# Layer 0 of a four-layer graph network: keys projected directly in turned form, their lengths moved into the exponentials, queries normed one block ahead

## The chip, the cores and the metric

The kernel runs on one core of a Trainium2 chip. The metric is the device time of one execution in microseconds (us). The kernel before takes 2383.84 us, the median of three runs from 2383.57 to 2384.07.

The engines are named as in the profile: PE does matmuls (PEld is its weight load), DVE is the vector engine, ACT the scalar engine, POOL is GpSimd, and SP issues nearly all transfers (DMA).

## The reference

Four layers are applied to 3327 nodes with 256 features each, under one 0/1 adjacency matrix. Each layer ends in a residual sum and a layer norm. All is fp32.

```python
# layer 0                                   x = layernorm(x + layer0(x, adj, Wq, Wk))
Qn = cos_normalize(x @ Wq.T)                # 3327 x 128, each row divided by max(its length, 1e-4)
Kn = cos_normalize(x @ Wk.T)
att = softmax(where(adj > 0, Kn @ Qn.T, -9e15), axis=1)
prop = att @ x                              # rows without a neighbour keep x
out = 0.5 * prop + 0.5 * x
# layer 1: graph attention, exp of leaky_relu(src_i + dst_j), times h = x @ W, then elu
# layer 2: scaled dot-product attention under the mask, q, k, v with biases, then elu
# layer 3: h = x @ W0, then three graph attention layers like layer 1
```

What matters here is layer 0. The row index i of the attention belongs to Kn and the summed index j to Qn. The kernel's code calls the i side queries and the j side keys, so its keys come from Wq and its queries from Wk. Each score is k_i . q_j / (|k_i| |q_j|).

## The kernel before

**Tiles and blocks.** The nodes are padded to 3328: 26 tiles of 128 (`NT`). A block (`b`) is four tiles, 512 rows of the attention; there are seven, the last with 256 rows. A group of tiles is the same four tiles seen as keys. Each of the six attention layers (`layers`: "0", "1", "2", "3a", "3b", "3c") is a loop over blocks, and in each block over the 26 key tiles `j`: one step of the flat list `steps`.

**One step of layer 0** (`weights0`, L438). PE multiplies the stationary `FT[j // 4][:, 0, ...]` (keys, turned: 128 features x 128 nodes) with the moving `FT[b][:, 1]` (queries, turned: 128 features x 512 nodes) into a PSUM bank `ps` (L444). ACT takes the exponential (`ex`, L453). DVE multiplies with the mask (`e`, L433). PE multiplies pieces of `e` with the features `V[0][j]` into four accumulators `po`. `make_to` makes steps ahead: while PE does the products of step `j`, the scores of step `j + 2` are made (`LA = 2`). For every second `j`, a 512 KB piece of the adjacency (`stage`, three buffers) has been loaded; DVE or ACT turn it into the byte mask, and DVE adds it up into `acc` (L405) to find rows without neighbours.

**Two forms of products.** Block 0 and the last block multiply plainly (L1253: four products of 257 columns a step). Blocks 1 to 5, and all of layer 2, use Strassen's scheme on pairs of tiles: `sums` makes four sums of `e` pieces on DVE (L656 to L659), `products` does 14 products of 128 or 129 columns a pair (L708). The sums of feature tiles that this needs (`tsum`) are made once per pair by `combine` (L629) on DVE, stored to memory (`t_d`, L640) and fetched again for each block (`fetch_tsum`, `tsums`, three buffers). In layer 0 `combine` runs at steps 9 to 21 of block 0; in layer 2 the sums of the last pair are made when the last block of layer 1 is finished, during block 0 of layer 2.

**Preparing layer 0** (`prep0(g)`, L286), a generator that is advanced a part at a time between the steps of block 0, for all seven groups. For each tile, two matmuls with `xT` stationary and 256 columns of weights moving give keys and queries side by side (`pqk`, L311); a copy brings them to SBUF (`qk`); ACT or DVE sum the squares (L302, L306); DVE takes the roots of eight columns at once (`rsqrt`, three Newton steps, eleven instructions, behind a maximum); DVE scales the queries (L346) and ACT the keys (L344); PE turns both (`pqkT`, L352) and ACT copies them to `FT` (L356). So every `ps` of a group stands behind its copy, squares, root, scaling and turn.

**Order.** Up to step 3 the order on PE, ACT, DVE and POOL is that of the program (`manual_schedule`). After that, and for SP throughout, Tile's scheduler orders each engine's instructions: by their place in the program, but by the times it expects for each, so an instruction it holds ready can be put ahead of one that it expects to wait. [...]The trace shows the effect on SP, where loads that the program issues in later blocks (`w_l_wq`, `a_3a`) stand at 33 to 40 us.

**Shared buffers.** The tag `x4k` has two buffers of 4 KB a partition. In block 0 of layer 0 it carries `xT` (the features turned, 512 KB a group) and the 13 `tsum` tiles; in later blocks of the layer it carries `y4`, the result that `finish` works on. The PSUM pool `ps_b` has three banks for everything except the accumulators.

Of the kernel before, what the change touches and what calls it, by code (L numbers as in the profile page):

```python
# [19 lines left out]
P = 128  # L20
D = 256
H = 128
# [11 lines left out]
def gnn_stack(ctx: ExitStack, tc: tile.TileContext, a: dict, N: int, out: bass.AP):  # L34
# [15 lines left out]
    def bw(b):  # L50
        return min(CH, NP - b * CH)

    def tiles_of(b):
        return range(4 * b, min(4 * b + 4, NT))
# [11 lines left out]
    def bank(name):  # L66
        return ps_b.tile([P, CH], F32, tag="pb", name=name)
# [61 lines left out]

    w = {}  # L130

    def rsqrt(dst, v, n):

        g = cols.tile([P, n], I32, tag="rs_g", name="rs_g")
        nc.vector.tensor_scalar(g, v.bitcast(I32), -0.5, MAGIC, ALU.mult, ALU.add)
        y = g.bitcast(F32)
        vh = cols.tile([P, n], F32, tag="rs_v", name="rs_v")
        nc.vector.tensor_scalar(vh, v, -0.5, None, ALU.mult)
        for k in range(3):
            q = cols.tile([P, n], F32, tag="rs_q", name="rs_q")  # L140
            nc.vector.tensor_tensor(q, y, y, ALU.mult)
            nc.vector.tensor_tensor(q, q, vh, ALU.mult)
            z = dst if k == 2 else cols.tile([P, n], F32, tag="rs_y", name="rs_y")
            nc.vector.scalar_tensor_tensor(z, q, 1.5, y, ALU.add, ALU.mult)
            y = z


# [123 lines left out]
    def load_xT(g):  # L271
        wd = bw(g)
        xT = work.tile([P, 2, CH], F32, tag="x4k", name="xT", bufs=2)
        src = a["xT"].rearrange("(h p) n -> p h n", p=P)
        if g == 0:
            for q, c in ((nc.scalar, 0), (nc.sync, D)):
                q.dma_start(xT[:, :, c : c + D], src[:, :, c : c + D])
        else:
            nc.sync.dma_start(xT[:, :, :wd], src[:, :, g * CH : g * CH + wd])
        xTs[g] = xT  # L280

    def load_x(g):
        for t in tiles_of(g):
            nc.sync.dma_start(V[0][t][:, :D], a["x"][t * P : (t + 1) * P, :])

    def prep0(g):  # L286

        wd = bw(g)
        xT = xTs[g]
        ts_ = tiles_of(g)  # L290
        ss = cols.tile([P, 2, 4], F32, tag="ss", name="ss")
        if len(ts_) < 4:
            nc.vector.memset(ss, 1.0)
        qks = []

        def squares(k):
            for i in range(2):
                s = qks[k][:, i * H : (i + 1) * H]
                c = ss[:, i, k : k + 1]
                jk = work.tile([P, H], F32, tag=f"sq{i}", name=f"sq{i}", bufs=1)  # L300
                if g < 2 and i == 1:
                    nc.vector.tensor_tensor_reduce(  # L302
                        jk, s, s, 1.0, 0.0, ALU.mult, ALU.add, c
                    )
                else:
                    nc.scalar.activation(jk, s, AF.Square, accum_out=c)  # L306

        for k, t in enumerate(ts_):
            pm = bank("pqk")
            for h in range(2):  # L310
                nc.tensor.matmul(  # L311
                    pm[:, : 2 * H],
                    xT[:, h, k * P : (k + 1) * P],
                    w["qk"][:, h, :],
                    start=(h == 0),
                    stop=(h == 1),
                )
            tag, bufs = ("y", 6) if g % 2 else ("qk", 4)
            qk = work.tile([P, 2 * H], F32, tag=tag, name="qk", bufs=bufs)
            if g in (1, 2):  # L320
                nc.scalar.copy(qk, pm[:, : 2 * H])
            else:
                nc.vector.tensor_copy(qk, pm[:, : 2 * H])
            qks.append(qk)
            if g == 0:
                squares(k)
        yield
        if g > 0:
            for k in range(len(ts_)):
                squares(k)  # L330
            yield

        sf = ss.rearrange("p i k -> p (i k)")
        nc.vector.tensor_scalar(sf, sf, COS_EPS * COS_EPS, None, ALU.max)
        rn = cols.tile([P, 8], F32, tag="rn", name="rn")
        rsqrt(rn, sf, 8)
        if g == 1:
            yield
        for k in range(len(ts_)):
            for i in (1, 0):  # L340
                s = qks[k][:, i * H : (i + 1) * H]
                c = rn[:, 4 * i + k : 4 * i + k + 1]
                if i == 0:
                    nc.scalar.mul(s, s, c)  # L344
                else:
                    nc.vector.tensor_scalar(s, s, c, None, ALU.mult)  # L346
        yield
        for i in (1, 0):
            pt = bank("pqkT")
            for k, t in enumerate(ts_):  # L350
                s = qks[k][:, i * H : (i + 1) * H]
                nc.tensor.transpose(pt[:, k * P : (k + 1) * P], s, ident)  # L352
            if i == 1 and g == 0:
                nc.vector.tensor_copy(FT[g][:, i, :wd], pt[:, :wd])
            else:
                nc.scalar.copy(FT[g][:, i, :wd], pt[:, :wd])  # L356


    masks = {}
# [78 lines left out]
    def weights0(b, j):  # L438
        wd = bw(b)
        if j % 2 == 0:  # L440
            take_adj(b, j)
            load_adj()
        ps = bank("ps")
        nc.tensor.matmul(  # L444
            ps[:, :wd],
            FT[j // 4][:, 0, (j % 4) * P : (j % 4 + 1) * P],
            FT[b][:, 1, :wd],
            start=True,
            stop=True,
        )  # L450
        t_ = work.tile([P, CH], F32, tag="a", name="ex", bufs=3)

        nc.scalar.activation(t_[:, :wd], ps[:, :wd], AF.Exp)  # L453
        return masked(b, j, t_)

    gq = {}
# [169 lines left out]
    def strassen(L, b):  # L626
        return L.key == "2" or (L.key == "0" and 0 < b < NB - 1)

    def combine(key, p, v):  # L629

        b1, b2 = v[2 * p], v[2 * p + 1]
        b11, b12, b21, b22 = b1[:, H:D], b1[:, :H], b2[:, H:D], b2[:, :H]
        t = work.tile([P, 4 * H + 1], F32, tag="x4k", name="tsum", bufs=2)
        t1, t2, t3, t4 = (t[:, c : c + H] for c in (0, H + 1, 2 * H + 1, 3 * H + 1))
        nc.gpsimd.memset(t[:, H : H + 1], 1.0)
        nc.vector.tensor_tensor(t1, b12, b11, ALU.subtract)
        nc.vector.tensor_tensor(t2, b22, t1, ALU.subtract)
        nc.vector.tensor_tensor(t3, b22, b12, ALU.subtract)
        nc.vector.tensor_tensor(t4, t2, b21, ALU.subtract)
        nc.sync.dma_start(t_d[key][p], t)  # L640

    tsums = {}

    def fetch_tsum(key, b, p):
        t = work.tile([P, 4 * H + 1], F32, tag="tsum", name="tsums", bufs=3)
# [499 lines left out]
    def make(s):  # L1145
        if s >= len(steps):
            return
        L, b, j = steps[s]
        if strassen(L, b) and j % 2 == 0:
            fetch_tsum(L.key, b, j // 2)  # L1150
        if L.is_gat:
            made.append(L.gat.weights(b, j))
        else:
            made.append((weights0 if L.key == "0" else weights2)(b, j))
            if strassen(L, b) and j % 2:
                e2, e1 = made.pop(), made.pop()
                made.append(None)
                made.append(sums(b, e1, e2))
# [10 lines left out]
    load_x(0)  # L1169
    load_adj()  # L1170
    masks[0] = new_mask(0)
    prep = [prep0(0), prep0(1)]
    next(prep[0])
    next(prep[1])
    next(prep[0])
    next(prep[0], None)
    for s in range(LA):
        make(s)
    prep.pop(0)
    setup = setups()  # L1180
    pre = iter(())

# [4 lines left out]
    def make_to(n):  # L1187
        nonlocal upto
        while upto < n:
            make(upto)  # L1190
            upto += 1

    for s, (L, b, j) in enumerate(steps):
# [8 lines left out]
            pos = [ps_o.tile([P, wo], F32, tag="po", name="po") for _ in range(no)]  # L1202
        if first:

            g, part = (j + 4) // 4, j % 4
            if part == 2 and g + 1 < NB:
                load_x(g + 1)
                if g + 2 < NB:
                    load_xT(g + 2)
                prep.append(prep0(g + 1))  # L1210
                next(prep[-1])
                if g > 1:
                    next(prep[-1])
                else:
                    next(prep[0])
                    next(prep.pop(0), None)
            if j == 3:
                next(prep[0])
            if g < NB and g > 1 and part < 2:
                next(prep[0], None)  # L1220
                if part == 1:
                    prep.pop(0)
        if j == 0 and first:
            load_x(1)
            load_xT(2)
            make_to(s + LA + 1)
            next(prep[0])
        elif j == 1 and first:
            make_to(s + LA + 1)
            next(prep[0])  # L1230
        else:
            make_to(s + LA + 1 + extra)
        es = None if end else made.popleft()
        if end:

# [139 lines left out]
```

## Time and profile before

| | |
|---|---|
| runs | 2383.57 to 2384.07 us, median 2383.84 |
| profiled execution | 2386.34 us |
| its span (first to last instruction) | 2384.6 us |
| PE busy | 2349.7 us, 99% |
| DVE, ACT, POOL busy | 1618.4, 1212.8, 13.5 us |
| layer 0: first `ps`, first `po`, end of block 0 | 16.2, 18.9, 121.1 us |
| blocks 2, 3, 4 of layer 0 | 63.0 us each |
| moved by DMA | 212.83 MB, 89 GB/s on average |

A busy PE in this profile is not PE at its peak: matmul lengths overlap, and their ends are modelled. The pace of a run of matmuls is read from the starts of successive runs. A line of the order of time gives start, length, engine, source line, operation, output and inputs with their shapes, the count, and in brackets the idle time before it with what ended it. An fp32 matmul of the program appears as two matmul instructions, a transpose as one.

### The profile page before, as it was taken

What the parts mean: (1) busy time and instruction counts of PE and PEld (TensorE: products, weight loads), DVE (VectorE), ACT (ScalarE), POOL (GpSimd) and SP (SyncE); (2) the same over time, 40 slices, a digit from 0 to 9 for tenths busy, and PEclk for the clock granted to TensorE, in tenths of its full rate; (3) what the DMA queues carried; (4) which work ended last, traced back from release to release, by engine and by line L of the source; (5) the groups of instructions that cost most, each with busy time, mean ns of one, the idle gap of its engine ahead of it and who ended that gap; (6) DMA issues with size and microseconds to landing.
All of it is one profiled execution on the core that took longest, in us unless ns stands there. A gap on an engine that the chain in (4) does not pass through costs nothing.

```text
span 2384.6 us, 33057 instructions
## 1 busy us (share of the span) xinstructions
PE 2349.7 (99%) x11911; PEld 1916.7 (80%) x11911; DVE 1618.4 (68%) x4353; ACT 1212.8 (51%) x1984; POOL 13.5 (1%) x91
## 2 busy tenths in 40 slices
PE   9999999999999999999999999999999999999997
PEld 6687777888888776677667798888888888888886
DVE  6789999966666657567467585556656555655665
ACT  5666666665555422222222255565655555655554
POOL 0000000000000000000000000000000000000000
PEclk9999999999999999999999999999999999999999
DMA  7556555523223322222212231111221111132120
GB/s 228 165 167 191 183 186 181 175 82 94 73 69 70 100 56 87 67 69 84 64 62 72 76 93 47 55 65 34 61 62 43 43 52 51 47 100 69 60 66 23
DMA packets 146232, 212.83 MB, mean 89 GB/s; under 512 B 76061, under 2 KB 100884, under 8 KB 141460
## 3 DMA queue, kind: packets, MB, share of 16 engines
q1 hardware_dynamic: 145796, 210.45, 29.3%
q8 instruction: 94, 1.54, 0.3%
q14 instruction: 70, 0.57, 0.1%
q10 hardware_dynamic: 272, 0.26, 0.0%
HBM read 165.70 MB, written 28.19 MB: 81 GB/s over the span
## 4 chain that ended last, share of the span: by engine, by line
PE 64%; DVE 2%; ACT 1%; DMA 1%; issue 0%; POOL 0%; POOLq 0%; DVEq 0%; ACTq 0%
PE po L1253 36%; PE ps L506 12%; PE po L708 11%; PE pproj L917 3%; DMA turned<-planes 1%; PE pgq L465 1%; PE po L1238 1%; ACT re L600 1%; DVE e L611 0%; PE pv L1002 0%; DVE v L611 0%; ACT planes L763 0%; DVE ejunk L534 0%; DVE pT L773 0%; DMA u<-s_d 0%
## 5 line engine op out<-in xcount | busy, mean ns | idle before, releaser
L1253 PE MATMUL po<-v,e 128*128 128x257 f32 x5616 | 1251.7, 381 | 2.5 <-ACT p L886 1.7
L1253 PEld LDWEIGHTS po<-v,e 128*128 128x128 f32 x5616 | 1063.2, 190 | 174.9 <-issue 15.2
L600 ACT ACTIVATE re<-u,nrh,th 128x512 f32<-128x512 f32 (+1 forms) x728 | 555.9, 780 | 478.4 <-DVE e L611 474.9
L611 DVE SCALAR_TENSOR_TENSOR e<-re,rh,mask 128x512 f32<-128x512 f32 (+1 forms) x702 | 502.4, 719 | 380.1 <-PE po L1253 360.5
L433 DVE SCALAR_TENSOR_TENSOR e<-ex,mask 128x512 f32<-128x512 f32 (+1 forms) x364 | 234.8, 649 | 183.7 <-ACT ex L514 157.0
L506 PE MATMUL ps<-gT,ft 128*128 128x512 f32 (+1 forms) x728 | 307.7, 563 | 0.0
L514 ACT ACTIVATE ex<-ps,off 128x512 f32<-128x512 f32 (+1 forms) x182 | 119.2, 655 | 360.3 <-PE ps L506 331.5
L708 PE MATMUL po<-tsums,ssum 128*128 128x128 f32 (+1 forms) x1794 | 250.1, 275 | 2.6 <-DVE ssum L658 1.3
L708 PEld LDWEIGHTS po<-tsums,ssum 128*128 128x128 f32 x1794 | 224.3, 192 | 5.1 <-DVE ssum L658 2.3
L708 PEld LDWEIGHTS po<-v,e 128*128 128x128 f32 x1196 | 169.7, 191 | 71.3 <-issue 53.6
L506 PEld LDWEIGHTS ps<-gT,ft 128*128 128x128 f32 x728 | 131.9, 190 | 113.6 <-issue 110.7
L708 PE MATMUL po<-v,e 128*128 128x129 f32 x1196 | 183.2, 275 | 0.0
L453 ACT ACTIVATE ex<-ps 128x512 f32<-128x512 f32 (+1 forms) x182 | 102.7, 564 | 119.8 <-PE ps L444 106.3
L444 PE MATMUL ps<-ft,ft 128*128 128x512 f32 (+1 forms) x312 | 143.6, 568 | 0.8 <-ACT ft L356 0.7
L405 DVE CUSTOM_DVE_ANT_0 acc<-acc,stage 128x1024 uint16<-128x1024 uint16 (+1 forms) x168 | 109.0, 649 | 13.8 <-DMA stage<-in_adj_a 9.8
L708 PE MATMUL po<-v,ssum 128*128 128x128 f32 x598 | 92.3, 275 | 0.0
L708 PE MATMUL po<-tsums,e 128*128 128x128 f32 x598 | 92.1, 275 | 0.0
L397 ACT ACTIVATE mask<-pos 128x1024 uint8<-128x1024 bf16 (+1 forms) x87 | 86.5, 994 | 2.5
L396 ACT ACTIVATE pos<-stage 128x1024 bf16<-128x1024 int32 (+1 forms) x87 | 85.8, 986 | 2.5 <-DVE e L433 2.4
L917 PE MATMUL pproj<-w_l_w,pT 128*128 128x256 f32 x304 | 77.9, 380 | 3.3 <-DVE pT L773 3.3
L708 PEld LDWEIGHTS po<-v,ssum 128*128 128x128 f32 x598 | 79.4, 192 | 0.1
L708 PEld LDWEIGHTS po<-tsums,e 128*128 128x128 f32 x598 | 79.3, 192 | 0.0
(218 smaller groups left out, 1722.6 us busy)
## 6 DMA issues: line engine op xcount, KB each, us to landing
mask<-mask_d SPq DMA_DIRECT2D x30, 1664.0 KB
tsums<-t_d SPq DMA_DIRECT2D x156, 256.5 KB
stage<-in_adj_a SPq DMA_DIRECT2D x78, 512.0 KB
mask_d<-mask SPq DMA_DIRECT2D x6, 1664.0 KB
t_d<-tsum SPq DMA_DIRECT2D x26, 256.5 KB
u<-s_d SPq DMA_DIRECT2D x24, 256.0 KB
mask<-mask_d SPq DMA_DIRECT2D x5, 832.0 KB
v<-in_x SPq DMA_DIRECT2D x26, 128.0 KB
```

Source lines behind the costliest of these rows:

```text
L397: nc.scalar.activation(mask(b, j, 2), t_[:, : 2 * wd], AF.Sign)
L405: nc.vector.tensor_tensor(acc, acc, st[:, h * wd : (h + 1) * wd], ALU.add)
L433: nc.vector.scalar_tensor_tensor(e[:, :wd], t_[:, :wd], 0.0, mask(b, j), ALU.add, ALU.mult)
L444: nc.tensor.matmul(ps[:, :wd], FT[j // 4][:, 0, (j % 4) * P : (j % 4 + 1) * P], FT[b][:, 1, :wd], start=True, stop=True,)
L453: nc.scalar.activation(t_[:, :wd], ps[:, :wd], AF.Exp)
L506: nc.tensor.matmul(ps[:, :wd], FT[j // 4][:, h, (j % 4) * P : (j % 4 + 1) * P], g[:, h, :wd], start=(h == 0), stop=(h == 1),)
L514: nc.scalar.activation(t_[:, :wd], ps[:, :wd], AF.Exp, bias=off, scale=1.0 / D**0.5)
L600: nc.scalar.activation(t_[:, :wd], self.u[b][:, :wd], AF.Relu, bias=self.nrh[:, j : j + 1], scale=self.th[:, j : j + 1],)
L611: nc.vector.scalar_tensor_tensor(e[:, :wd], t_[:, :wd], self.rh[:, j : j + 1], mask(b, j), ALU.add, ALU.mult,)
L708: nc.tensor.matmul(o, x, y, start=(p == 0 and g not in banks[:i]), stop=(p == NT // 2 - 1 and g not in banks[i + 1 :]),)
L917: nc.tensor.matmul(pm[:, :D], pT[:, h, :], w[L.w][:, h, :], start=(h == 0), stop=(h == 1),)
L1253: nc.tensor.matmul(pos[k], es[:, k * P : (k + 1) * P], V[L.i % 2][j], start=(j == 0), stop=(j == NT - 1),)
```

## The change

1. **Keys** (`keys0(g)`) are projected directly into turned form: the weights are stationary and `xT` moves, so two matmuls of 512 columns give 128 features x 512 nodes (`pq`). ACT squares them into `qsq` and copies them, not normed, to `FT[g][:, 0]`. The squared lengths come from PE: each tile of `qsq` is the stationary operand of a matmul with one column of ones (`pn0`). DVE takes the roots into a column of `rq`. The lengths are no longer multiplied into the keys: the exponential takes `rq[:, j]` as its per-partition scale.
2. **Queries** (`queries0(b)`) are still normed and turned (`pk`, `kr`, `pkT`), but each group only one block before its block: during block 0 from step 18 for group 1, during blocks 1 to 5 from step 10 for the next. Their roots run on POOL (`lengths` with `nc.gpsimd`), except for group 0. `xT` of that group is loaded a second time, at step 14 of block 0 and at step 6 of the others.
3. `rsqrt` takes an engine; on POOL its fused last operation is two, so a root with its maximum is fifteen instructions there.
4. The loads of block 0 are spaced differently: `load_xT` of groups 3 to 6 at steps 4, 8, 12, 16 in place of 2, 6, 10, 14.
5. **Last pair's sums**: in layer 2, `combine` of the last pair writes to a tile of the tag `tsum`, which block 0 uses without fetching it. The store stays, for the other blocks.

The removed `prep0` is printed above; it is cut here.

```diff
-    def rsqrt(dst, v, n):
...
+    def rsqrt(dst, v, n, eng=nc.vector, tag="rs"):
+        g = cols.tile([P, n], I32, tag=tag + "_g", name="rs_g")
+        eng.tensor_scalar(g, v.bitcast(I32), -0.5, MAGIC, ALU.mult, ALU.add)
...
+            eng.tensor_tensor(q, y, y, ALU.mult)
+            eng.tensor_tensor(q, q, vh, ALU.mult)
+            z = dst if k == 2 else cols.tile([P, n], F32, tag=tag + "_y", name="rs_y")
+            if eng is nc.vector:
+                eng.scalar_tensor_tensor(z, q, 1.5, y, ALU.add, ALU.mult)
+            else:
+                eng.tensor_scalar(q, q, 1.5, None, ALU.add)
+                eng.tensor_tensor(z, q, y, ALU.mult)
...
-    def prep0(g):
...
+    rq = const.tile([P, NT], F32, name="rq")
+
+    def lengths(dst, v, n, eng=nc.vector, tag="rs"):
+        eng.tensor_scalar(v, v, COS_EPS * COS_EPS, None, ALU.max)
+        rsqrt(dst, v, n, eng, tag)
+
+    def keys0(g):
+        wd, n = bw(g), len(tiles_of(g))
+        xT = xTs[g]
+        pm = bank("pq")
+        for h in range(2):
+            nc.tensor.matmul(
+                pm[:, :wd], w["qk"][:, h, :H], xT[:, h, :wd], start=(h == 0), stop=(h == 1)
+            )
+            if g == 1 and h == 0:
+                yield
+        yield
+        sq = work.tile([P, CH], F32, tag="u", name="qsq", bufs=2)
+        nc.scalar.activation(sq[:, :wd], pm[:, :wd], AF.Square)
+        nc.scalar.copy(FT[g][:, 0, :wd], pm[:, :wd])
+        yield
+        pn = bank("pn0")
+        for k in range(n):
+            nc.tensor.matmul(
+                pn[:, k : k + 1], sq[:, k * P : (k + 1) * P], ones[:, :1], start=True, stop=True
+            )
+        yield
+        v = cols.tile([P, 4], F32, tag="qss", name="qss")
+        nc.vector.tensor_scalar(v[:, :n], pn[:, :n], COS_EPS * COS_EPS, None, ALU.max)
+        rsqrt(rq[:, 4 * g : 4 * g + n], v[:, :n], n)
+
+    def queries0(g):
+        wd, n = bw(g), len(tiles_of(g))
+        xT = xTs[g]
+        ss = cols.tile([P, 4], F32, tag="kss", name="kss")
+        kr = work.tile([P, 4, H], F32, tag="kr", name="kr", bufs=1)
+        banks = [bank("pk") for _ in range(2 if g == 0 else 1)]
+        for k in range(n):
+            pk = banks[k // 2 if g == 0 else 0][:, k * H : (k + 1) * H]
+            for h in range(2):
+                nc.tensor.matmul(
+                    pk,
+                    xT[:, h, k * P : (k + 1) * P],
+                    w["qk"][:, h, H:],
+                    start=(h == 0),
+                    stop=(h == 1),
+                )
+        if g > 0:
+            nc.scalar.copy(kr.rearrange("p k n -> p (k n)")[:, :wd], banks[0][:, :wd])
+            yield
+        src = [
+            banks[k // 2][:, k * H : (k + 1) * H] if g == 0 else kr[:, k, :] for k in range(n)
+        ]
+        for k in range(n):
+            jk = work.tile([P, H], F32, tag="sq0", name="sq", bufs=1)
+            nc.scalar.activation(jk, src[k], AF.Square, accum_out=ss[:, k : k + 1])
+        yield
+        rk = cols.tile([P, 4], F32, tag="rk", name="rk")
+        if g == 0:
+            lengths(rk[:, :n], ss[:, :n], n)
+        else:
+            lengths(rk[:, :n], ss[:, :n], n, nc.gpsimd, "prs")
+        yield
+        for k in range(n):
+            if g == 0 and k >= 2:
+                nc.vector.tensor_scalar(kr[:, k, :], src[k], rk[:, k : k + 1], None, ALU.mult)
             else:
...
+                nc.scalar.mul(kr[:, k, :], src[k], rk[:, k : k + 1])
+        yield
+        pt = bank("pkT")
+        for k in range(n):
+            nc.tensor.transpose(pt[:, k * P : (k + 1) * P], kr[:, k, :], ident)
+        nc.scalar.copy(FT[g][:, 1, :wd], pt[:, :wd])
...
-        nc.scalar.activation(t_[:, :wd], ps[:, :wd], AF.Exp)
+        nc.scalar.activation(
+            t_[:, :wd], ps[:, :wd], AF.Exp, scale=rq[:, j : j + 1]
+        )
...
-        t = work.tile([P, 4 * H + 1], F32, tag="x4k", name="tsum", bufs=2)
+        here = key == "2" and p == NT // 2 - 1
+        if here:
+            t = work.tile([P, 4 * H + 1], F32, tag="tsum", name="tsums", bufs=3)
+            tsums[0, p] = t
+        else:
+            t = work.tile([P, 4 * H + 1], F32, tag="x4k", name="tsum", bufs=2)
...
-        if strassen(L, b) and j % 2 == 0:
+        if strassen(L, b) and j % 2 == 0 and (L.key, b, j) != ("2", 0, NT - 2):
             fetch_tsum(L.key, b, j // 2)
...
-    prep = [prep0(0), prep0(1)]
...
+    k0, q0, q1 = queries0(0), keys0(0), keys0(1)
+    for part in (k0, q0, k0, q0, q0, k0, k0, q0, q1):
+        next(part, None)
+    make(0)
+    next(q1)
+    make(1)
+    prep = deque()
+    kprep = iter(())
...
-            g, part = (j + 4) // 4, j % 4
-            if part == 2 and g + 1 < NB:
...
+            if j == 0:
+                load_x(1)
+                load_xT(2)
+            elif j % 4 == 2 and j < 20:
+                load_x((j + 6) // 4)
+            elif j % 4 == 0 and j < 20:
+                load_xT((j + 8) // 4)
+        make_to(s + LA + 1 + extra)
+        if first:
+            if j < 2:
+                next(q1)
+                if j == 1:
+                    next(q1, None)
+            elif j % 4 == 2 and j < 20:
+                prep.append(keys0((j + 6) // 4))
+            if prep:
                 next(prep[0], None)
...
+                if j % 4 == 0:
+                    next(prep.popleft(), None)
+        if L.key == "0" and b < NB - 1:
+            at = 14 if b == 0 else 6
+            if j == at:
+                load_xT(b + 1)
+            elif j == at + 4:
+                kprep = queries0(b + 1)
+            if j >= at + 4:
+                next(kprep, None)
...
```

More of the change, by code (lines that the diff above doesn't have):

```diff
@@ L130, in gnn_stack @@
     w = {}
-    def rsqrt(dst, v, n):
-        g = cols.tile([P, n], I32, tag="rs_g", name="rs_g")
-        nc.vector.tensor_scalar(g, v.bitcast(I32), -0.5, MAGIC, ALU.mult, ALU.add)
+    def rsqrt(dst, v, n, eng=nc.vector, tag="rs"):
+        g = cols.tile([P, n], I32, tag=tag + "_g", name="rs_g")
+        eng.tensor_scalar(g, v.bitcast(I32), -0.5, MAGIC, ALU.mult, ALU.add)
         y = g.bitcast(F32)
-        vh = cols.tile([P, n], F32, tag="rs_v", name="rs_v")
-        nc.vector.tensor_scalar(vh, v, -0.5, None, ALU.mult)
+        vh = cols.tile([P, n], F32, tag=tag + "_v", name="rs_v")
+        eng.tensor_scalar(vh, v, -0.5, None, ALU.mult)
         for k in range(3):
[L140 to L144, printed above, removed]
+            q = cols.tile([P, n], F32, tag=tag + "_q", name="rs_q")
+            eng.tensor_tensor(q, y, y, ALU.mult)
[6 more added lines that the diff above has]
+                eng.tensor_tensor(z, q, y, ALU.mult)
             y = z
@@ L284, in load_x @@
             nc.sync.dma_start(V[0][t][:, :D], a["x"][t * P : (t + 1) * P, :])
-    def prep0(g):
-        wd = bw(g)
-        xT = xTs[g]
[L290 to L309, printed above, removed]
+    rq = const.tile([P, NT], F32, name="rq")
@@ L310, in prep0 @@
+    def queries0(g):
[6 more added lines that the diff above has]
+            pk = banks[k // 2 if g == 0 else 0][:, k * H : (k + 1) * H]
             for h in range(2):
                 nc.tensor.matmul(
-                    pm[:, : 2 * H],
+                    pk,
@@ L313, in prep0 @@
                     xT[:, h, k * P : (k + 1) * P],
-                    w["qk"][:, h, :],
+                    w["qk"][:, h, H:],
                     start=(h == 0),
@@ L317, in prep0 @@
                 )
[L318 to L321, printed above, removed]
-            else:
[L323 to L326, printed above, removed]
+        if g > 0:
+            nc.scalar.copy(kr.rearrange("p k n -> p (k n)")[:, :wd], banks[0][:, :wd])
+            yield
@@ L327, in prep0 @@
+        yield
+        for k in range(n):
+            if g == 0 and k >= 2:
+                nc.vector.tensor_scalar(kr[:, k, :], src[k], rk[:, k : k + 1], None, ALU.mult)
+            else:
+                nc.scalar.mul(kr[:, k, :], src[k], rk[:, k : k + 1])
         yield
[L328 to L356, printed above, removed]
+        pt = bank("pkT")
@@ L627, in strassen @@
         return L.key == "2" or (L.key == "0" and 0 < b < NB - 1)
+    tsums = {}
     def combine(key, p, v):
@@ L640, in combine @@
         nc.sync.dma_start(t_d[key][p], t)
-    tsums = {}
     def fetch_tsum(key, b, p):
@@ L1171, in gnn_stack @@
     masks[0] = new_mask(0)
-    prep = [prep0(0), prep0(1)]
[L1173 to L1179, printed above, removed]
+    k0, q0, q1 = queries0(0), keys0(0), keys0(1)
[6 more added lines that the diff above has]
+    kprep = iter(())
     setup = setups()
@@ L1203, in gnn_stack @@
         if first:
-            g, part = (j + 4) // 4, j % 4
-            if part == 2 and g + 1 < NB:
[L1207 to L1219, printed above, removed]
-                next(prep[0], None)
[L1221 to L1232, printed above, removed]
+            if j == 0:
[14 more added lines that the diff above has]
+            if prep:
+                next(prep[0], None)
+                if j % 4 == 0:
[8 more added lines that the diff above has]
+                next(kprep, None)
         es = None if end else made.popleft()
```

## The prediction

> **What bounds the kernel now.** I read the page first, then the waits of the first layer, the order of time on PE, and busy time by stage.
>
> ```profile
> PE 2349.7 (99%) x11911; PEld 1916.7 (80%) x11911; DVE 1618.4 (68%) x4353; ACT 1212.8 (51%) x1984; POOL 13.5 (1%) x91
> ```
>
> PE is busy for all but 35 us of 2384.6. So an edit pays only by taking instructions off PE, or by removing one of PE's rare stops. By stage (columns: stretch, PE, PEld, DVE, ACT and POOL busy, clock, DMA share, GB/s):
>
> ```profile
> 16.20:35.00 18.80, 18.01 (x69) 12.62 (x70) 15.42 (x43) 10.96 (x40) 0.00 (x0) 1.00 0.82 250
> 80.00:121.10 41.10, 35.86 (x139) 25.55 (x138) 28.25 (x97) 22.85 (x44) 0.79 (x8) 0.96 0.56 177
> 184.00:247.00 63.00, 62.66 (x418) 50.28 (x418) 61.76 (x171) 42.90 (x58) 0.00 (x0) 1.00 0.61 186
> ```
>
> The first two lie in block 0 of layer 0, where PE stops; the third is one later block, where PE is full, DVE nearly so (61.8 of 63.0), and ACT has 20 us to spare. The stops, in the order of time on PE (start, length, what, the idle time before it):
>
> ```profile
> 37.70 0.67 PE L1253 MATMUL po<-v,e 128*128 128x257 f32 x2 [0.22 <-issue]
> 40.70 1.71 PE L352 MATMUL pqkT<-ident,qk 128*128 128x128 f32 x7 [2.33 <-ACT qk L344]
> 42.21 1.92 PE L444 MATMUL ps<-ft,ft 128*128 128x512 f32 x2
> 43.91 0.39 PE L352 MATMUL pqkT<-ident,qk 128*128 128x128 f32 x1
> 44.13 1.48 PE L1253 MATMUL po<-v,e 128*128 128x257 f32 x6
> 45.44 3.62 PE L311 MATMUL pqk<-w_l_wqk,xT 128*128 128x256 f32 x16
> 48.89 1.02 PE L444 MATMUL ps<-ft,ft 128*128 128x512 f32 x2
> 49.75 1.90 PE L1253 MATMUL po<-v,e 128*128 128x257 f32 x8
> 51.49 1.02 PE L444 MATMUL ps<-ft,ft 128*128 128x512 f32 x2
> ...
> 105.45 1.10 PE L352 MATMUL pqkT<-ident,qk 128*128 128x128 f32 x4 [2.81 <-DVE qk L346]
> 106.34 1.92 PE L444 MATMUL ps<-ft,ft 128*128 128x512 f32 x2
> ```
>
> [...]Eight `po` take 51.49 - 49.75 = 1.74 us (0.217 each), two `ps` 0.86, sixteen `pqk` 3.45 (0.216 each), eight transposes 0.87 elsewhere (0.109 each). Twice PE waits for a transpose's input, and the next `ps` pair then takes 1.92 in place of 1.02. The waits of the first 122 us (total, times, longest):
>
> ```profile
> DVE acc L405 <- DMA stage<-in_adj_a: 7.8, 7, 1.9
> ...
> PE pqkT L352 <- ACT qk L344: 3.8, 2, 2.3
> ...
> PE pqkT L352 <- DVE qk L346: 3.0, 2, 2.8
> ```
>
> Block 0 runs from its first `po` (18.86) to the block's end (121.1): 102.3 us. Its work: 26 steps x (1.74 + 0.86) = 67.5; `pqk` of groups 2 to 6, 72 x 0.216 = 15.5; 44 transposes, 4.8; row sums and weight products 1.3. Sum 89.1, so 13.2 us are stops: 8.5 idle, the rest slow instructions behind it.
>
> **What the skill says.** The Trainium skill, "TensorE: Matmul & The Clock Gate", Part 1: an idle PE falls to half clock, for about 3.4 us of work. Here 2.3 us of waiting is enough, and about 1.8 us is lost per stop. "ScalarE: Activation LUTs", What ACT_TABLE_LOAD costs: a pointer operand adds about 93 ns to an ACTIVATE. The trace agrees, 686 against 597 ns (exp with and without a bias column):
>
> ```profile
> L514 ACT ACTIVATE ex<-ps,off 128x512 f32<-128x512 f32 x136 | 93.3, 686 | 295.9 <-PE ps L506 268.8 <-DVE xsum L785 16.6 <-DVE p L750 6.4
> L453 ACT ACTIVATE ex<-ps 128x512 f32<-128x512 f32 x128 | 76.4, 597 | 90.7 <-PE ps L444 77.3 <-DVE ssum L658 6.5 <-DVE ssum L659 4.1
> ```
>
> "SBUF — State Buffer", Who interferes with whom: a GpSimd instruction that reads SBUF and a DVE instruction with two SBUF inputs (or in a two-port mode) lock each other out for a whole instruction. Before has no small reading instruction on POOL, but the lock shows: one memset takes 0.10 us alone, and 1.23 beside a DVE copy of 1.37 for two.
>
> ```profile
> 565.79 1.23 POOL L635 MEMSET tsum<- 128x1 f32 x1 [14.66 <-DMA turned<-planes]
> 603.23 0.10 POOL L635 MEMSET tsum<- 128x1 f32 x1 [36.21 <-PE pproj L917]
> ```
>
> **The change part by part.**
>
> *Start.* Before, the first exp runs at 17.34, behind square sums (to 11.07), DVE's root (2.2 us), scalings, and two turns and copies (to 16.1). After, group 0 needs 16 instructions of 128 columns (1.8 us in place of 3.5), four squares (0.43 us apart) to about 9.5, the root to about 12, scaling 0.5 to 0.7, one turn and one copy (0.45 + 0.58): `ps` at about 13.9. But exp now also waits for the second root (DVE, 12.5 to 14.9), and DVE then has the first mask and count (1.3 us) before `e`. First `po` at about 16.9 in place of 18.86: -2.0 us.
>
> *Block 0, PE work.* Removed: `pqk` 15.5 and transposes 4.8. Added: projections of groups 2 to 6, 4 x 4 x 0.43 + 4 x 0.216 = 7.7; length sums of groups 1 to 6, 22 tiles x 2 instructions; the like (128x128 weights, two columns, L153) take 0.10 each: 4.4; queries of group 1, 16 x 0.111 (the pace of 128-column products in later blocks) + 4 x 0.109 = 2.2. New work: 67.5 + 7.7 + 4.4 + 2.2 + 1.3 = 83.1. Without any stop the block gains 102.3 - 83.1 = 19.2 us.
>
> *Stops that stay.* The two waits above vanish: no transpose and no root stands ahead of `ps` any more for the keys; the root only gates exp, two steps (5.2 us) later, and takes 2.4. What is late next is data. DVE still waits for `stage` (7.8 us in all), and for stores that free the two-buffer tag `x4k`. The loads of groups 3 to 6 are now issued two steps before use in place of four; two `stage` loads issued at 29.3 landed at 33.9 and 36.3, so such a load can take 4.5 to 7 us under traffic and PE would stand behind it. One more load (group 1 again) holds one of the two `x4k` buffers for four steps while the 13 `tsum` tiles pass, and on SP stands ahead of `stage` loads and `tsum` stores. Bounds: 0 to 13 us. I take 5, below half of today's, as DVE loses 18 copies of 0.42, 26 scalings of 0.22 and 8 squares of 0.37 (16 us) and can catch up.
>
> *Blocks 1 to 5, PE.* Each norms the next group's queries: 2.2 us on PE; half (8 x 0.111 + 2 x 0.109 = 1.1) for group 6. Nothing hides it, PE being full: 4 x 2.2 + 1.1 = +10.0 us. On ACT, copies, squares and scalings add 4.7 us a block and the pointer 26 x 0.09 = 2.3, under 20 us of idle; without that cover it would be 7 us a block. One load of 512 KB a block, issued four steps (9.7 us) ahead, at DMA share 0.6: nothing.
>
> *Roots on POOL.* 15 dependent instructions on 128x4. Low: 0.10 each, the memset alone, 1.5 us. High: each waits for one DVE instruction of 0.42 to 0.69 (nearly all of DVE's have two SBUF inputs): 15 x 0.65 = 9.8. ACT's scalings wait in order behind them, with every later exp and mask behind those on ACT, and DVE and PE behind exp; then PE's transposes wait, with the products behind. From squares to transposes there are about two steps (4.84 us) and a bit, less four scalings (1.3): some 4 us of cover. DVE loses 15 x 0.1 = 1.5 us, and gets the 2.2 that PE adds. I take 4.3 us, a wait of 0.3 in five blocks: +1.5; ends 0 and 5 x 6 = 30.
>
> *Last pair's sums.* In layer 2 PE waits once for the pair's way through memory; it now reads the tile where DVE wrote it (916.3 to 917.8, 11 us earlier): -1.3 us.
>
> ```profile
> 929.82 1.61 PE L708 MATMUL po<-tsums,ssum 128*128 128x128 f32 x12 [1.27 <-DMA tsums<-t_d]
> ```
>
> **Sum**, against this execution's span of 2384.6: -2.0 - 19.2 + 5 + 10.0 + 1.5 - 1.3 = -6.0 us. The execution's own time was 2386.34, 1.7 outside the span; the runs' median is 2383.84. The same difference gives 2377.8.
>
> **Rivals.**
> *No stops at all.* PE pays only for its work: -6.0 - 5 - 1.5 = -12.5, 2371. For it: later blocks run with stops of 0.34 us. Against: DMA at 0.8 to 1.0 in the first 40 us.
> *Block 0 keeps its stops.* Loads two steps ahead, and `x4k` shared with `tsum`, stop PE for as long as the root did: -6.0 + 8.2 = +2.2, 2386. For it: DVE's wait for `stage`, and the last stop of before, where the root was strung out from 98.9 to 105.1 between `tsum` pieces that waited for stores. Against: `ps` no longer needs the root.
> *POOL becomes the bound (slower).* At 15 x 0.45 = 6.8 us the transposes wait 2.8, and the half clock takes 1.8: 4.6 x 5 = 23 in place of 1.5: +15.5, 2399. It decides from (6.0 + 1.5) / 5 = 1.5 us a block, roots of 5.5 us or 0.37 each. For it: the lock, DVE full just in those steps. Against: POOL does nothing else there; after step 3 a planner orders each engine's work by its own times and may place transposes later.
>
> **How the numbers follow.** Chances: forecast 0.45, no stops 0.16, stops stay 0.20, POOL 0.19. A measurement of this kernel can tell about 0.2% (4.8 us) from no change. The forecast's own range is 2373 to 2382, and some three quarters of it lie below 2379.0. Faster: 0.34 + 0.16 + 0.05 of the third case = 0.55; same: 0.11 + 0.12 + 0.01 = 0.24; slower: 0.03 + 0.18 = 0.21. The range runs from 2369 to 2393: it leaves out the POOL case's upper half and the best of the second.
>
> **What would show it.** First `po` near 16.9; block 0 some 83 us of work and 5 of stops, no wait for `qk`; blocks 1 to 4 near 65.2 us each in place of 63.0; exp near 690 ns; no wait at `tsums` in layer 2. I would be wrong by a PE wait at `pkT` behind `kr` (POOL), a PE wait for `xT`, or POOL rows above 0.37 us start to start.

## The result, and the profile after

The changed kernel takes 2401.57 us (median of 6 runs, 2397.49 to 2408.57) where the kernel before took 2383.57 beside it: a ratio of 1.0081, 95% interval [1.0066, 1.0096]. It is slower by some 18 us, outside the predicted range. The profiled execution took 2401.12 us, its span was 2399.3. The spans of the two traces differ by 14.7 us only, as the profiled execution of the kernel before (2386.34) lies 2.8 above that median.

The first line of the page, of the changed kernel, has 54 more instructions on PE and 7.7 us more of PE's busy time, and POOL with 33 us of work that it did not have:

```profile
PE 2357.4 (98%) x11965; PEld 1920.3 (80%) x11965; DVE 1607.1 (67%) x4305; ACT 1223.1 (51%) x1952; POOL 46.8 (2%) x181
```

Where the time went shows by stage. I cut at the same events in both kernels: the first `po`, the first product of block 1, and the transposes of the neighbour count (`pasum`), which come once a block. Block 1 and two later blocks of the kernel before (columns: stretch, its length, then busy time of PE, PEld, DVE, ACT and POOL, clock, DMA share, GB/s):

```profile
121.93:186.71 64.78, 64.78 (x430) 52.63 (x430) 56.70 (x149) 42.08 (x63) 0.00 (x0) 1.00 0.57 180
186.71:251.28 64.57, 64.23 (x425) 51.13 (x424) 62.45 (x172) 43.71 (x59) 0.00 (x0) 1.00 0.62 191
251.28:315.84 64.56, 64.22 (x424) 51.12 (x423) 62.63 (x172) 43.70 (x59) 0.00 (x0) 1.00 0.59 186
```

Block 0 and then the same three blocks of the changed kernel:

```profile
17.84:111.24 93.40, 86.62 (x355) 63.32 (x354) 62.17 (x195) 48.51 (x75) 5.64 (x28) 0.96 0.67 207
111.24:181.08 69.84, 67.44 (x450) 54.76 (x450) 56.95 (x148) 47.68 (x77) 3.79 (x15) 1.00 0.53 172
181.08:252.23 71.15, 68.30 (x443) 54.16 (x443) 63.06 (x172) 48.83 (x73) 6.34 (x15) 0.98 0.53 175
252.23:323.62 71.39, 68.55 (x445) 54.32 (x443) 62.94 (x172) 48.83 (x73) 6.33 (x15) 0.98 0.53 176
```

So, before to after: first `po` 18.86 to 17.84 (-1.0); block 0 from 103.1 to 93.4 (-9.7); block 1 from 64.8 to 69.8 (+5.1); blocks 2, 3 and 4 (the last from its own two `pasum`, 64.69 to 71.44) +6.6, +6.8 and +6.8; block 5, whose next group is half as wide, 64.6 to 67.1 (+2.5); block 6 +0.2; all that follows, 1901.6 to 1899.1 (-2.5). The sum of these rounded parts is +14.8, against 2399.3 - 2384.6 = 14.7 of the spans. Block 0 gained two thirds of the 14.2 us forecast for it, and the five blocks behind it lost nearly three times its gain.

PE in the order of time, of the changed kernel, with two stops in block 0 and, below, the one of block 2 with the two `ps` pairs ahead of it:

```profile
79.62 1.72 PE L305 MATMUL pq<-xT,w_l_wqk 128*128 128x256 f32 x4 [3.20 <-DMA xT<-in_xT]
81.14 3.02 PE L335 MATMUL pk<-w_l_wqk,xT 128*128 128x128 f32 x16
...
99.42 0.62 PE L366 MATMUL pkT<-ident,kr 128*128 128x128 f32 x2 [3.58 <-ACT kr L362]
...
218.65 1.02 PE L455 MATMUL ps<-ft,ft 128*128 128x512 f32 x2
...
222.64 1.02 PE L455 MATMUL ps<-ft,ft 128*128 128x512 f32 x2
225.91 0.33 PE L366 MATMUL pkT<-ident,kr 128*128 128x128 f32 x1 [2.24 <-ACT kr L362]
226.77 1.06 PE L366 MATMUL pkT<-ident,kr 128*128 128x128 f32 x3 [0.54 <-ACT kr L362]
227.62 1.91 PE L455 MATMUL ps<-ft,ft 128*128 128x512 f32 x2
229.33 1.23 PE L726 MATMUL po<-v,e 128*128 128x129 f32 x6
```

PE stands 2.78 us behind the scaled queries (`kr`), and the next `ps` pair takes 1.91 in place of 1.02. The same stop comes again 71 us later, and 71 us after that. Who was late is read in three timelines of the same microseconds. POOL, the start of its root and its end:

```profile
218.02 3.48 POOL L296 TENSOR_SCALAR kss<-kss 128x4 f32<-128x4 f32 x1 [67.49 <-ACT sq L350]
221.58 0.20 POOL L135 TENSOR_SCALAR rs_g<-kss 128x4 int32<-128x4 int32 x1
...
225.22 0.20 POOL L148 TENSOR_TENSOR rk<-rs_q,rs_y 128x4 f32<-128x4 f32 x1
```

DVE:

```profile
220.12 0.69 DVE L444 SCALAR_TENSOR_TENSOR e<-ex,mask 128x512 f32<-128x512 f32 x1
220.72 0.69 DVE L416 CUSTOM_DVE_ANT_0 acc<-acc,stage 128x1024 uint16<-128x1024 uint16 x1
226.46 0.69 DVE L444 SCALAR_TENSOR_TENSOR e<-ex,mask 128x512 f32<-128x512 f32 x1 [5.05 <-ACT ex L464]
```

ACT:

```profile
218.75 0.69 ACT L464 ACTIVATE ex<-ps,rq 128x512 f32<-128x512 f32 x1 [0.81 <-PE ps L455]
...
225.45 0.40 ACT L362 ACTIVATE kr<-kr,rk 128x128 f32<-128x128 f32 x1 [5.88 <-POOL rk L148]
225.76 0.67 ACT L464 ACTIVATE ex<-ps,rq 128x512 f32<-128x512 f32 x1
```

POOL's first instruction, the `max`, takes 3.48 us for 128x4 elements. It ends (221.50) when DVE's last instruction ends (221.41) and DVE has nothing more to do. The other 14 then pass at 0.28 us start to start. DVE has run dry because the next exp stands on ACT behind the scaling, the scaling waits for POOL, and POOL waits for DVE. That the exp stands behind the scaling can be read too: PE had the `ps` of 218.65 done at 219.67, and the next exp starts at 225.76, after the scaling of 225.45. The root takes 7.4 us in place of the 4.3 forecast. From the waits of the first 450 us (total, times, longest):

```profile
DVE e L444 <- ACT ex L464: 43.7, 28, 5.1
ACT kr L362 <- POOL rk L148: 26.5, 5, 5.9
PE pkT L366 <- ACT kr L362: 11.9, 7, 3.6
...
PE pq L305 <- DMA xT<-in_xT: 3.2, 1, 3.2
```

### The profile page after: what moved, and what is told of

Read it like the earlier page. It is cut to its first block, busy times and chain, and to the rows that moved or that the text cites. A ratio compares the mean times of both kernels' runs of the same rounds, so it can differ in the third digit from the quotient of the medians.

```text
span 2399.3 us, 33184 instructions
## 1 busy us (share of the span) xinstructions
PE 2357.4 (98%) x11965; PEld 1920.3 (80%) x11965; DVE 1607.1 (67%) x4305; ACT 1223.1 (51%) x1952; POOL 46.8 (2%) x181
## 4 chain that ended last, share of the span: by engine, by line
PE 87%; DVE 4%; DMA 3%; ACT 2%; issue 1%; POOL 1%; SPq 0%; POOLq 0%; DVEq 0%; ACTq 0%
PE po L1271 46%; PE po L726 17%; PE ps L519 12%; PE ps L455 4%; PE pproj L935 3%; DMA stage<-in_adj_a 1%; DMA turned<-planes 1%; PE pv L1020 1%; PE pgq L478 1%; ACT re L613 1%; PE po L1256 1%; POOL kss L296 0%; DVE ejunk L547 0%; DVE e L444 0%; DVE acc L416 0%
## 5 line engine op out<-in xcount | busy, mean ns | idle before, releaser
L464 ACT ACTIVATE ex<-ps,rq 128x512 f32<-128x512 f32 (+1 forms) x182 | 118.8, 653 | 117.8 <-PE ps L455 110.2
```

The source lines that it names most:

```text
L464: nc.scalar.activation(t_[:, :wd], ps[:, :wd], AF.Exp, scale=rq[:, j : j + 1])
```

## Experiments

Theory 1: the root on POOL, held off by DVE, stops ACT, then DVE, then PE. Theory 2: the work added to full blocks does it, whoever takes the root. Theory 3, for the smaller rest: block 0's data come late. Ratios are to the kernel before, run beside each; the changed kernel stood at 1.0081.

**Root on DVE** (label e1_roots_dve).

```diff
-            lengths(rk[:, :n], ss[:, :n], n, nc.gpsimd, "prs")
+            lengths(rk[:, :n], ss[:, :n], n, nc.vector, "prs")
```

> Theory 1 (the root on POOL): in blocks 2 to 4 the stop at pkT, its half clock and nothing else make 8.3 - 2.2 = 6.1 us each, and block 0's stop behind kr some 5 more; with the root on DVE these go: about 2378 us (2372 to 2386), blocks 2 to 4 near 65 to 66 us each, no wait of ACT's kr, no wait of PE's pkT above 1 us. Theory 2 (the added work of PE and ACT in full blocks, whoever takes the root): 2399 to 2404, blocks still 71 us.

Measured: 2386.44 us, ratio 1.0006 [0.9997, 1.0014]. This one word is worth 15 to 18 us (by the medians and by the ratios). Blocks 2 to 4 take 67.2, 67.6 and 67.2 us. The waits of PE for the scaled queries fall from 11.9 us to this:

```profile
PE pkT L366 <- ACT kr L362: 2.3, 3, 0.8
```

Theory 2 falls. The absolute time expected was 8 us too low. It held the blocks against the forecast's 63.0 us, which was the width of a window and not a block's period. The period is 64.6, so it counted 1.6 us a block too much as recoverable, and a block was to take some 67 here.

**Nobody waits for POOL** (label e2_no_wait), the sharpest test of why POOL is slow.

```diff
-                nc.scalar.mul(kr[:, k, :], src[k], rk[:, k : k + 1])
+                nc.scalar.mul(kr[:, k, :], src[k], rk[:, k : k + 1] if g == 0 else 0.1)
```

> The queries are scaled by a constant in place of their root, so the root on POOL is still computed but nobody waits for it; the queries' norm is left out. Theory 1, with DVE's two-input instructions as what holds POOL: DVE no longer runs dry, so the first POOL instruction of a root lasts longer than the 3.5 us of the changed kernel, until DVE happens to idle (10 us or more in some blocks), and yet the time falls to 2374 to 2382, as no one waits. Rival within it (POOL is slow by itself after a long rest): the first instruction again lasts 3.5 us in every block and the root 7.4. Theory 2: 2399 to 2404.

Measured: 2382.41 us, ratio 0.9989 [0.9983, 0.9996]. POOL's timeline in the third block, where the changed kernel had 3.48:

```profile
219.07 15.59 POOL L296 TENSOR_SCALAR kss<-kss 128x4 f32<-128x4 f32 x1 [64.44 <-ACT sq L350]
```

And DVE's, at that instruction's end:

```profile
233.50 0.73 DVE L416 CUSTOM_DVE_ANT_0 acc<-acc,stage 128x1024 uint16<-128x1024 uint16 x1
234.11 0.47 DVE L676 TENSOR_TENSOR ssum<-ssum,e 128x256 f32<-128x256 f32 x1
234.61 0.42 DVE L677 TENSOR_TENSOR ssum<-e,ssum 128x256 f32<-128x256 f32 x1
235.60 0.69 DVE L444 SCALAR_TENSOR_TENSOR e<-ex,mask 128x512 f32<-128x512 f32 x1 [0.56 <-ACT ex L464]
```

From 219.1 to 234.6 DVE starts one instruction with two inputs in SBUF after another, each ahead of the former's recorded end. Then come 234.11 + 0.47 = 234.58 and the next start at 234.61, the first break since POOL's `max` began; it ends at 234.66. The next two blocks have 15.70 and 15.53, and there too POOL's instruction ends 0.08 us after the end of the DVE instruction with the first break behind it. So in these three blocks POOL does not take turns with DVE: it gets none until DVE has a break. In the changed kernel the wait was only 3.5 us because POOL's own lateness, by way of ACT, starved DVE.

This is not so wherever DVE runs on. In block 5 of the changed kernel, with DVE's instructions as close together, POOL gets its turn at the end of one DVE instruction after another, though no break lies between them. POOL, and DVE beside it:

```profile
427.96 0.41 POOL L296 TENSOR_SCALAR kss<-kss 128x2 f32<-128x2 f32 x1 [60.03 <-ACT sq L350]
428.45 0.22 POOL L135 TENSOR_SCALAR rs_g<-kss 128x2 int32<-128x2 int32 x1
428.74 0.56 POOL L138 TENSOR_SCALAR rs_v<-kss 128x2 f32<-128x2 f32 x1
```

```profile
427.87 0.41 DVE L674 TENSOR_TENSOR ssum<-e 128x256 f32<-128x256 f32 x1
428.20 0.40 DVE L675 TENSOR_TENSOR ssum<-e 128x256 f32<-128x256 f32 x1
428.54 0.67 DVE L416 CUSTOM_DVE_ANT_0 acc<-acc,stage 128x1024 uint16<-128x1024 uint16 x1
429.14 0.41 DVE L676 TENSOR_TENSOR ssum<-ssum,e 128x256 f32<-128x256 f32 x1
```

That root takes 6.6 us, and e2_no_wait and e13_less_dve have the like in their block 5. So a POOL instruction that meets such a run of DVE is either let in behind the instruction under way or held off until the next break. What decides between the two, the runs do not show.

Blocks 2 to 4 of e2_no_wait take 66.2, 66.8 and 66.5 us, +1.9 over before on average, and that is the added work without a stop at `pkT`.

**DVE with breaks** (label e13_less_dve).

```diff
-            for h in range(2):
+            for h in range(0 if 1 <= b <= 4 and 8 <= j <= 16 else 2):
```

> The changed kernel, root on POOL, with ten of DVE's two-input count instructions taken out of the middle of each of blocks 1 to 4 (source tiles 8 to 16 are left out of the neighbour count), 6 us of DVE's 64 a block. Theory 1 (POOL gets no turn while DVE runs such instructions without a pause): DVE now pauses, the first POOL instruction of a root lasts under 1.5 us in place of 3.5, PE's stop at pkT shrinks from 2.8 us to under 1, and blocks 2 to 4 take 66 to 68 us: 2383 to 2390. If the length of the first POOL instruction has another cause (a rest of 65 us before it), it stays at 3.5 and the blocks at 71: 2397 to 2403.

Measured: 2391.28 us, ratio 1.0044 [1.0028, 1.0059]; blocks 2 to 4 take 68.0 to 68.2. POOL, again in the third block:

```profile
216.87 0.22 POOL L296 TENSOR_SCALAR kss<-kss 128x4 f32<-128x4 f32 x1 [67.48 <-ACT sq L350]
```

DVE stands idle for 1.10 us here, just as POOL begins. After the same rest of 67.5 us the first instruction takes 0.22 in place of 3.48. Its rest is not the cause; DVE's unbroken run is. PE's stop at `pkT` falls from 2.78 us to 0.54, and the blocks by 3.2 us each. ACT still waits out the root of 4.8 us, so they do not come down to 66.5. The time is a little above the 2383 to 2390 expected.

**A constant scale for exp** (label e4_scale_imm).

```diff
-            t_[:, :wd], ps[:, :wd], AF.Exp, scale=rq[:, j : j + 1]
+            t_[:, :wd], ps[:, :wd], AF.Exp, scale=0.1
```

> The changed kernel with exp scaled by a constant in place of the keys' factor column (the keys' lengths are computed but left out of the result). ACT saves 156 x 0.09 = 14 us, some 2.3 us a block. Theory 1: ACT's load is not what stops PE, so the blocks stay at 71 us: 2399 to 2402, the start perhaps 1 us earlier as exp no longer waits for the root. Theory 2 (ACT's added work): a fall by 5 us or more, below 2397.

Measured: 2404.93 us, ratio 1.0081 [1.0068, 1.0095], as the changed kernel. The 0.09 us that the factor column costs each exp is hidden, and the first `po` comes no earlier (18.48). This run also has POOL held off in block 5, with the same order of DVE instructions as in the changed kernel's, where it was let in; the block takes 72.1 us in place of 67.1:

```profile
429.04 6.19 POOL L296 TENSOR_SCALAR kss<-kss 128x2 f32<-128x2 f32 x1 [59.93 <-ACT sq L350]
```

**The last pair's sums alone**, on the kernel before (label e3_sums_only).

```diff
-        t = work.tile([P, 4 * H + 1], F32, tag="x4k", name="tsum", bufs=2)
+        here = key == "2" and p == NT // 2 - 1
+        if here:
+            t = work.tile([P, 4 * H + 1], F32, tag="tsum", name="tsums", bufs=3)
+            tsums[0, p] = t
...
-        if strassen(L, b) and j % 2 == 0:
+        if strassen(L, b) and j % 2 == 0 and (L.key, b, j) != ("2", 0, NT - 2):
```

> The kernel before with the last pair's sums kept, nothing else. The sum had -1.3 us: 2382.3 in place of 2383.6, and no wait of PE at tsums in the third layer's first block. Rival (the wait moves to the next late operand): 0 us.

Measured: 2384.36 us, ratio 0.9995 [0.9987, 1.0003]: too small for the timed runs to tell. The trace tells it. The wait is gone, and from layer 2's first `pn` to its first row transpose (`psr`) PE takes 970.46 - 817.70 = 152.76 us in place of 973.12 - 818.81 = 154.31: -1.55. The changed kernel has 152.81.

**Block 0's data.** Five kernels, all with the root on DVE. First, `xT` loaded four steps ahead (label e6_dve_early):

```diff
-            elif j % 4 == 2 and j < 20:
+            elif j % 4 == 2 and j < 18:
                 load_x((j + 6) // 4)
-            elif j % 4 == 0 and j < 20:
-                load_xT((j + 8) // 4)
+                load_xT((j + 10) // 4)
+            elif j == 18:
+                load_x((j + 6) // 4)
```

> Roots on DVE, and block 0's loads of xT issued four steps before use, as the kernel before did, in place of two. Theory 3 (what is left against the forecast is the data's lateness in block 0): PE's stop of 3.6 us at pq behind xT and the half clock behind it (16 pk in 3.0 us in place of 1.8) go: 4.8 us below the same kernel with the late loads, 2380 to 2383. Rival: two xT tiles then hold both x4k buffers while the tsum pieces pass, and DVE waits there: no gain, 2385 to 2388.

Measured: 2381.13 us, ratio 0.9992 [0.9984, 1.0000], 3 us below e1_roots_dve by the ratios and 5 by the medians. The stop at `pq` is gone, and block 0 takes 86.4 us in place of 90.0. Smaller stops follow (1.32 us at `pkT`, 0.96 at `pasum`).

Then the pieces of `tsum` in buffers of their own, with the change's load times (label e8_dve_own):

```diff
-            t = work.tile([P, 4 * H + 1], F32, tag="x4k", name="tsum", bufs=2)
+            tag, bufs = ("tsum", 3) if key == "0" else ("x4k", 2)
+            t = work.tile([P, 4 * H + 1], F32, tag=tag, name="tsum", bufs=bufs)
```

> Roots on DVE, loads of xT as in the change, but block 0's tsum pieces in buffers of their own. If the load is late because its buffer comes free only with a tsum store (it was issued 2.3 us after the queue's last store), the stop at pq shrinks from 3.6 us to some 1 us, and DVE's waits for tsum stores go: 2381 to 2384. If the load is late because it is issued too late or the DMA engines are loaded, the stop stays above 3 us.

Measured: 2379.51 us, ratio 0.9990 [0.9982, 0.9998]. The stop at `pq` is gone: the load is issued at 71.95 in place of 77.50 (e1_roots_dve; 76.72 in the changed kernel). So the shared buffer made it late. DVE's waits for `tsum` stores did not go (6.3 us, four times), and in place of the old stop PE stops once for the weights `e`, as DVE waits 6.5 us for a `stage` load:

```profile
72.97 3.51 PE L1272 MATMUL po<-v,e 128*128 128x257 f32 x8 [3.10 <-DVE e L444]
```

Both together (label e9_dve_early_own):

> Roots on DVE, loads of xT four steps ahead and tsum pieces in buffers of their own: no stop at pq and no wait of DVE for a tsum store in block 0, block 0 in 84 to 86 us from its first po: about 2379 (2377 to 2382), faster than both kernels.

Measured: 2379.78 us, ratio 0.9992 [0.9984, 1.0000]. Block 0, from its first `po`:

```profile
20.84:104.73 83.89, 83.30 (x355) 60.86 (x354) 59.50 (x196) 48.40 (x75) 0.99 (x10) 1.00 0.72 226
```

This is block 0 with hardly a stop, 83.9 us, though DVE still waits 5.5 us in all for `tsum` stores. But its first `po` comes at 20.84. With buffers free, Tile's scheduler put the first `tsum` pieces ahead of the first root on DVE, and they wait there 2.4 us for their rows of x. PE's clock (the clock column of such a line) also stood at 0.50 for longer ahead of `po`: 6.8 us, and 3.4 in e1_roots_dve. Of the 6.1 us that block 0 gained on e1_roots_dve, 2.6 are lost in front, and that it is faster than the kernel before is not certain.

Last, on top of that, the squares under the keys' lengths in bf16 (label e11_bf16_sums; the column of ones likewise):

```diff
-        sq = work.tile([P, CH], F32, tag="u", name="qsq", bufs=2)
+        sq = work.tile([P, CH], BF16, tag="u", name="qsq", bufs=2)
```

> As the last one, with the squares of the keys rounded to bf16 ahead of their length sums, so that each of the 26 sums is one matmul instruction in place of two. The sum priced 44 instructions of the 5 later groups and group 1 at 0.1 us each, 4.4 us; half of it goes, -2.2 us against the kernel without it: about 2377. Rival: the sums are covered or are bound by their weight load, 0 us.

Measured: 2378.37 us, ratio 0.9981 [0.9975, 0.9988]. Against the kernel without it -1.4 us in the medians, within the intervals of both. The traces settle the price of the sums: in block 0 of e9_dve_early_own they hold PE for 4.4 us, as forecast (44 instructions, 0.10 us each), and here for 0.6 (22 of 0.026). But PE's idle time in the block rises from 0.6 us to 4.0, and the block is no shorter (84.15 us). The same with the change's `tsum` buffers (label e14_early_bf16):

> Roots on DVE, loads of xT four steps ahead, length sums in bf16, tsum pieces in the buffers of the change. The kernels with tsum buffers of their own began some 3 us later (first po at 19.3 to 20.8 in place of 17.3 to 18.2), as DVE then stood early behind tsum's inputs; here the start should be near 17.3 again, against stops of some 2 us later in block 0: 2377 to 2380, about as the best so far.

Measured: 2378.23 us, ratio 0.9980 [0.9973, 0.9986]. The first `po` came at 18.77, not 17.3; in this trace PE's clock stood at 0.50 for 3.4 us ahead of it, and in that of e6_dve_early, where 17.3 comes from, it did not. These two are the fastest, 4.4 to 4.8 us faster than the kernel before and some 23 us below the change.

Not tried: the root on POOL with more steps between it and the scalings.

## Why the prediction was wrong

**Roots on POOL: the step that failed.** The forecast took 4.3 us for a root, 4 us of cover, and 1.5 us in all for five blocks. The bound of 9.8 us came from letting each of the 15 instructions wait for one DVE instruction. In blocks 2 to 4 neither is what happens. The first waits for all of DVE's instructions until DVE breaks off, 3.5 us here and 15.6 where nothing starves DVE, and the rest then run freely at 0.28. The root is 7.4 us long, PE idles 2.78 and with the slow instructions behind that loses 71.3 - 66.5 = 4.8 us a block (blocks 2 to 4 against e2_no_wait), 14.5 in three. The cover was about right: 7.4 - 2.78 = 4.6 us. It was the length of the root that was mis-sized. In block 1 DVE ran dry as POOL began (0.26 us); in block 5 POOL took turns with DVE (0.41).

The count was wrong too. The change makes six roots on POOL, as group 1's falls into block 0; the forecast counted five. In block 0 the root took 5.7 us, though its first instruction took only 0.70, and PE stopped 3.58 us behind the scaling.

The slower rival had the place, the chain and nearly the sum (6.8 us a root, 4.6 a block, 2399), at a chance of 0.19. That its sum came so near is in part luck: it gave every instruction 0.45 us, which fits block 5 alone (15 in 6.6 us), and in blocks 2 to 4 it is one wait of 3.5. What was missing was where DVE breaks off. That could have been read in the profile of before. These are all of DVE's rows there, from 186 to 252 us, that the timeline marks with idle time ahead of them:

```profile
188.84 0.69 DVE L433 SCALAR_TENSOR_TENSOR e<-ex,mask 128x512 f32<-128x512 f32 x1 [0.20 <-ACT ex L453]
197.37 0.89 DVE L851 SCALAR_TENSOR_TENSOR y<-v,c,y 128x256 f32<-128x256 f32 x2 [0.20 <-ACT y L839]
243.28 0.69 DVE L433 SCALAR_TENSOR_TENSOR e<-ex,mask 128x512 f32<-128x512 f32 x1 [0.64 <-ACT ex L453]
248.12 0.69 DVE L433 SCALAR_TENSOR_TENSOR e<-ex,mask 128x512 f32<-128x512 f32 x1 [0.88 <-ACT ex L453]
```

From 197.4 to 242.2, for 45 us, not one row starts after the end of the row ahead of it; from 218.8 on all of them have two inputs in SBUF. The root was put in the middle of that (218.0).

The Trainium skill, "SBUF — State Buffer", Who interferes with whom, says that a DVE instruction with two SBUF inputs contends with a GpSimd instruction that reads SBUF, that the shared ports are an exclusive lock, and that issue order decides who blocks. The traces agree that they exclude each other, but show more: over 15.6 us DVE took the next turn every time, and in block 5 the two alternated. "Perfetto Trace Analysis", Optimizing Scalar/DVE Operations, says that moving work between DVE and GpSimd might not help, for that shared port. Here it cost 15 to 18 us.

**Start: about right, as far as single traces tell.** The first `e` is ready at 16.88, where 16.9 was forecast for `po`. But PE has group 1's projection and two more `ps` in its order ahead of `po`, to 17.84, and its clock stood at 0.50 from 11.70 to 15.11. The trace of e13_less_dve, whose PE has the same order up to there, was at full clock in this stretch. First the changed kernel, then e13_less_dve:

```profile
11.70:15.11 3.41, 3.41 (x7) 1.61 (x6) 2.89 (x14) 0.59 (x1) 0.00 (x0) 0.50 0.93 326
11.70:15.11 3.41, 3.41 (x9) 1.36 (x8) 3.13 (x12) 1.25 (x2) 0.00 (x0) 1.00 0.87 300
```

There the first `po` is at 15.85. On the other side, e3_sums_only, which starts as the kernel before does, has it at 17.82 in place of 18.86. So the gain of 1.0 between two traces is no measure of the 2.0 forecast. That exp waits for the second root was no limit in the changed kernel: DVE wrote `rq` at 13.69, and exp went on waiting for `ps` until 15.47; without that wait (e4_scale_imm) `po` is no earlier.

**Block 0, PE work: right.** 83.1 us were worked out; e9_dve_early_own has 83.9 with hardly a stop. That the waits for the keys' root and turns would vanish was right.

**Stops that stay: right in kind.** Of the 5 us, `xT` two steps ahead and the shared buffers were named. They cost 3.2 us of stop and 1.1 in the 16 `pk` behind it (2.86 us from their start to the next run's, for 1.78 at the start of the kernel); e6_dve_early and e8_dve_own each take that stop away. Block 0 took 5 us more than the 88.1 forecast (93.4). The root accounts for most of it: 3.58 us of stop and 0.9 in the `ps` pair behind it. With the root on DVE the block falls by 3.4, as PE then stops 1.7 at `pasum`.

**Blocks 1 to 5, PE work: right in size.** 2.2 us a block were forecast, +1.9 measured (e2_no_wait, blocks 2 to 4), and +1.2 for 1.1 in block 5. Only the base was wrong: a block's period is 64.6 us, not 63.0. Block 1 takes 3.1 more in e2_no_wait; 0.7 of it is a wait at `pasum`, the rest was not traced to a cause.

**ACT's added work: right.** Exp takes 0.69 us with the factor column, and taking that off again changes nothing. Nor do the +1.9 us a block of e2_no_wait, which PE's added work fills, leave room for it.

**Last pair's sums: right.** -1.3 forecast, -1.55 in the trace of the kernel that has this alone.

**What is left.** Without the root's term the forecast was 7.5 us below the kernel before; e2_no_wait, which leaves that term out, is 2.6 below (0.9989). Its trace, of an execution 4.7 us above its median, puts the rest in front: the start gains 0.8 for 2.0, with PE's clock at 0.50 for 3.4 us, and block 0 takes 96.1 us for 88.1, as PE stops there 3.9 us for `xT` and 4.4 for the neighbour count at `pasum`, behind DVE. Without any stop the forecast was 12.5 below. In e9_dve_early_own block 0 is as worked out, but the start is 2 us later than before in place of 2 earlier, and DVE's roots cost 0.78 us of stop in three blocks. Its trace ends 5.9 us earlier than that of before; its timed runs say 0 to 3.8. Some 2 us of the difference is the choice of execution: the profiled one lies 2.8 us above its median in the kernel before, and 0.8 in e9_dve_early_own.

## What to carry to other kernels

Before moving small work to POOL, look at whether DVE has breaks in that stretch; a DVE that runs two-input instructions back to back can hold POOL off for as long as it goes on, and the average on the page (DVE 68% before) does not show such a stretch. It may also let POOL in, as block 5 shows, so count on neither. Then ask who stands in order behind the consumer: here one scaling on ACT held up every exp, which starved DVE and only thereby let POOL in. A buffer tag shared between a load and short-lived pieces can make the load wait for a piece's store: here it was issued some 5 us later than with buffers of their own.

## What was not expected of the hardware

A POOL instruction on 128x4 elements lasted 15.6 us beside DVE instructions of 0.4 to 0.7 us, and 0.2 us without them; a break of DVE of 0.03 us, ahead of a sum that takes the result of the one before it, let it in. In block 5 the same kind of instruction got in without any break in one execution (0.41 us) and was held off in another (6.19).

PE's clock stood at 0.50 for 3.41 us (226.73 to 230.14) from the end of its stop of 2.78 us, which made the next `ps` pair take 1.91 us in place of 1.02. After stops of 0.54 us (e13_less_dve) and 0.78 (e1_roots_dve) it stayed at 1.00. After a stop of 1.16 us at the start it fell in the changed kernel and did not in e13_less_dve.
